# Two-layer metaformer on one core: layer 0's expert tiles store their results under the tile's own number, the fetches read only their image's part, and a power of the preparation runs on VectorE

## The chip, the cores and the metric

The kernel runs on one core of a Trainium2 chip. A core has five engines with instruction queues of their own, each worked off strictly in order: TensorE (PE in the profile; PEld is its weight load), VectorE (DVE), ScalarE (ACT), GpSimd (POOL) and SyncE (SP, which here only issues transfers). POOL also issues transfers: the indirect ones, which read or write one row per index, and here the stores of layer 0's results. The metric is the device time of one execution in microseconds; lower is better.

## What is computed

Four images of 256 channels by 32 x 32 pixels go through two layers. Layer 0 is a top-k attention with a depthwise convolution, added to its input, and then a mixture of experts: every token (pixel) goes to the two best of eight small two-matrix networks, and their weighted results are added to it. Layer 1 is a selective scan over four directions, prepared by a normalization and a softplus, added to its input, and then a second mixture of experts with wider networks.

```python
x = x + _L0_conv_ref(_ln_c(x), ...)          # attention
t = _to_tokens(x)
t = t + _L0_ffn_ref(_ln_t(t), ...)           # layer 0's experts, top 2 of 8
x = _from_tokens(t, x)
x = x + _L1_conv_ref(_ln_c(x), ...)          # selective scan, 16 states
t = _to_tokens(x)
x = _from_tokens(t + _L1_ffn_ref(_ln_t(t), ...), x)   # layer 1's experts
```

## The kernel before, in words

**Stages.** By the lines in the trace: attention up to about 1910 us, routing of layer 0 to 2050, layer 0's experts from 2050 to 2296, the scans to about 3563, layer 1's experts and the output to the end.

**Routing (L1123 to L1230, called at L1474 to L1490).** For each image DVE normalizes, finds the two best experts of each token, and counts. Each expert owns a region of 16 blocks of 256 rows in the DRAM tensor slots_x0; a token's slot is its expert's region plus its rank among that expert's tokens. The two slot numbers per token (slot0) are cast to integers, and POOL scatters the tokens there, 16 indirect transfers an image, two for each group of 128 tokens (L1486). After the last image, fill_in_phases (L1091) lays out the order of the tiles, 256 rows each: first those that hold tokens of image 0, then of image 1, then of images 2 and 3. Its constants make at most 15 tiles (FIRST) enough for image 0 and 23 (SECOND) for images 0 and 1; 36 tiles (USUAL) run always, three more only if needed.

**Layer 0's experts (Tile0, L1499 to L1566, loop at L1589).** For each tile SP loads its rows (xs, 6 buffers) and its expert's two matrices (4 buffers); PE transposes (tp, L1523) and DVE copies the result (xe, L1525); PE multiplies (hp, L1545), ACT applies Gelu (L1547), PE multiplies again (yp, L1553); DVE adds the bias (ys, 8 buffers, L1556), ACT scales (L1560), DVE adds the token itself where this is its best expert (L1561). POOL then reads the tile's block number into a register and stores ys to that block of slots_y0 (L1564), so that a result lies at the slot of its token.

**What runs beside the tiles (L1581 to L1600).** Two generators are advanced four steps after each tile. The first starts at tile 15: it fetches image 0's results by its slots (fetched, L1425: 8 plain indirect transfers for the tokens' first expert, then 8 that add the second one; four a step, so all within one tile), lets 20 steps pass, has PE transpose them (op, L1447) and DVE add them to x (L1454). Then it goes on with the preparation of image 0's scan (Prep.steps, L1332): mean (L1341), variance (L1353), the variance plus epsilon (ve, L1356), its power -0.5 on POOL (ln_r, L1359), one Newton step on DVE (ln_rr and ln_rs, L1361 to L1364), its spreading by PE (ln_rb, L1371), two projections (bp, zp), and a softplus in halves of 512 columns: Relu, Abs and Exp on ACT (L1405 to L1407) for each of four parts, rounding losses on DVE (lost, L1395), one Ln (L1411). The second generator starts at tile 23 and does for image 1 what the first began with. Images 2 and 3 are fetched during the first scans, one transfer at a time.

**What sets the order.** In this stage the framework orders the instructions of each engine: program order is the priority, and its own estimate of what is ready decides who goes first; it also puts in the waits, by the parts of tensors that instructions read and write. Where an address comes from a register or from indices, the part is whatever the slice that was handed over covers; slots_y0 was always handed over whole. In attention and scans the order is the program's, written out by hand; preparation of images 1 to 3 is advanced there twice a scan, beside POOL's products (uu, L1678, and da_c, L1711) and DVE's scans (h, L1691, L1700, L1717).

**Zeros.** Slots that no token fills must be finite, so SP fills slots_x0 and slots_y0 with zeros during attention (L831, at turns 20 and 36).

Of the kernel before, what the change touches and what calls it, by code (L numbers as in the profile page):

```python
# [52 lines left out]
WIN = 7  # L53
ROOT_BITS = float(0x1FBB4F2E)
WIDE = 256.0
FIRST_DVE = (3, 2)
# [5 lines left out]
def metaformer(ctx: ExitStack, tc: tile.TileContext, t: dict, out: bass.AP):  # L62
# [73 lines left out]
    slots_x0 = dram.tile([(E * BLOCKS + 1) * T, W0], F32, tag="slots_x0", name="slots_x0")  # L136
    slots_y0 = dram.tile([(E * BLOCKS + 1) * T, C], F32, tag="slots_y0", name="slots_y0")
    results = dram.tile([2 * B * L + 2 * P, C], F32, tag="results", name="results")
# [10 lines left out]
    with ExitStack() as st:  # L149
# [644 lines left out]
        with tc.manual_schedule():  # L794
            norms = [normed(b) for b in range(B)]
            gates = [gated(b) for b in range(B)]
            lead = [groups[0, 0].steps(pause=True), images[0].values(0)]

            def beside_norms():

                while lead[0] is not None:
                    went = next(lead[0], "end")
                    if went is None:
                        lead.append(lead.pop(0))
                        if lead[0] is None:
                            return
                    if went == "end":
                        lead[0] = None
                    if went is True:
                        return  # L810

            for i in range(B + 2):
                for b in range(B):
                    if 0 <= i - b < 3:
                        next(norms[b], None)
                if i >= 2:
                    beside_norms()
            for gate in gates:
                for _ in range(3):
                    next(gate, None)  # L820
                    beside_norms()
            while lead[0] is not None:
                beside_norms()
            aim, aim_lo, aim_hi, z, half_z, rate, ends = thresholds()
            for _ in lead[1]:
                pass
            start(0)
            for i in range(len(order) + 8):
                if i in (20, 36):
                    wide_by = W0 if i == 20 else C  # L830
                    nc.sync.dma_start((slots_x0 if i == 20 else slots_y0).rearrange("(a p) c -> p a c", p=P),  # L831
                                      zeros[:, :wide_by].unsqueeze(1).to_broadcast(
                                          [P, (E * BLOCKS + 1) * T // P, wide_by]))
                if i == 3:
                    nc.sync.dma_start(slots_x.rearrange("(a p) c -> p a c", p=P),
                                      zeros[:, :W].unsqueeze(1).to_broadcast([P, (E * BLOCKS + 1) * T // P, W]))
                turn(i)
            due(1 << 20)
# [221 lines left out]
    class Tiles:  # L1060
# [30 lines left out]
        def fill_in_phases(self, room, upto, psum, tag):  # L1091
# [11 lines left out]
            nc.vector.tensor_tensor(base, homes.rearrange("p k e -> p (k e)"), ends, ALU.subtract)  # L1103
            nc.vector.tensor_tensor(base, base, upto, ALU.add)
            nc.vector.tensor_tensor(leap[:, : V - 1], base[:, 1:], base[:, : V - 1], ALU.subtract)
            nc.vector.memset(leap[:, V - 1 :], float(E * BLOCKS))
# [15 lines left out]

    def route(b, layer, tok, slot, space, psum, tag):  # L1123

# [12 lines left out]
        wide = [P, NT, E]  # L1137
        eq, hot1, hot2 = room([NT, E]), room([NT, E]), room([NT, E])
        red, m1, m2 = room([NT]), room([NT]), room([NT])
# [61 lines left out]
        nc.vector.tensor_tensor(place, place, tote, ALU.subtract)  # L1201
        nc.vector.tensor_tensor(place, place, count.unsqueeze(2).to_broadcast([P, E, NT]), ALU.add)
        nc.vector.tensor_tensor(place, place, region.unsqueeze(2).to_broadcast([P, E, NT]), ALU.add)
        nc.vector.tensor_tensor(count, count, cum[:, :, NT - 1], ALU.add)
# [113 lines left out]
    dsk = load(sw, "dskip", [P, CT])  # L1318
    power = sw.tile([P, NT], F32, tag="power", name="power")
    nc.gpsimd.memset(power, -0.5)  # L1320

    class Prep:
# [9 lines left out]
        def steps(self, room, psum, tag):  # L1332
# [15 lines left out]
            for h in range(NHALF):  # L1348
# [8 lines left out]
                if h == 0:  # L1357
                    yield
            nc.gpsimd.tensor_tensor(r0, ve, power, ALU.pow)  # L1359
            yield  # L1360
            nc.vector.tensor_tensor(rr, r0, r0, ALU.mult)  # L1361
            nc.vector.tensor_tensor(rr, rr, ve, ALU.mult)
            nc.vector.tensor_scalar(rr, rr, -0.5, 1.5, ALU.mult, ALU.add)
            nc.vector.tensor_tensor(rs, r0, rr, ALU.mult)  # L1364
            yield
# [31 lines left out]

            for i, (c, cols) in enumerate(parts):
                zp = psum.tile([P, HALF], F32, tag=tag, name="zp")
                for k in range(CT):  # L1400
                    nc.tensor.matmul(zp, wd[:, k, ts(c, P)], xm[:, k, cols], start=(k == 0), stop=(k == CT - 1))
                if i:
                    lost(*parts[i - 1])
                yield
                nc.scalar.activation(self.delta[:, c, cols], zp, AF.Relu, bias=bd[:, c : c + 1])  # L1405
                nc.scalar.activation(v[:, c, cols], zp, AF.Abs, bias=bd[:, c : c + 1])
                nc.scalar.activation(v[:, c, cols], v[:, c, cols], AF.Exp, scale=-1.0)  # L1407
                yield
            lost(*parts[-1])
            yield  # L1410
            nc.scalar.activation(v, v, AF.Ln, bias=1.0)  # L1411
            yield
# [11 lines left out]

    def fetched(b, y, halves, times=1):  # L1425

        issued = 0
        for k in range(2):
            for h in halves:
                for i in range(4):  # L1430
                    n = b * NT + h * 4 + i
                    nc.gpsimd.indirect_dma_start(
                        out=y[h][:, i], out_offset=None, in_=slots_y0,
                        in_offset=bass.IndirectOffsetOnAxis(ap=slot0[:, k, n : n + 1], axis=0),
                        compute_op=ALU.add if k else ALU.bypass)
                    issued += 1
                    if issued % times == 0:
                        yield

# [17 lines left out]
    def pause(times):  # L1457
        for _ in range(times):
            yield

    with ExitStack() as st:
# [4 lines left out]
            "p (e d) -> p e d", e=E))  # L1466
        pw = st.enter_context(tc.tile_pool(name="m0_e", bufs=4))
        with ExitStack() as sr:
            pr = sr.enter_context(tc.tile_pool(name="r0_w", bufs=1))
# [3 lines left out]
            scattered = nc.alloc_semaphore("scattered")  # L1473
            for b in range(B):  # L1474
                d = pd.tile([P, CT, L], F32, tag="d", name="d")
                here = slot0[:, :, ts(b, NT)]
                for _ in norm(b, 0, tokens[b], pd, ps_n, "t", "t", d):
                    pass
                numbers = pr.tile([P, 1408], F32, tag="numbers", name="numbers")
                for _ in route(b, 0, tokens[b], here, numbers, ps_n, "t"):  # L1480
                    pass
# [14 lines left out]
        ps_h = st.enter_context(tc.tile_pool(name="m0_ps_h", bufs=2, space=PSUM))  # L1496
        blocks_x, blocks_y = (a.rearrange("(k a p) c -> k p a c", a=T // P, p=P) for a in (slots_x0, slots_y0))

        class Tile0:  # L1499
# [58 lines left out]
            def store(self):  # L1558
                for a in range(T // P):
                    nc.scalar.mul(self.ys[:, a], self.ys[:, a], self.wt[:, a : a + 1])  # L1560
                    nc.vector.scalar_tensor_tensor(self.ys[:, a], self.xs[:, a, :C], self.best[:, a : a + 1],  # L1561
                                                   self.ys[:, a], ALU.mult, ALU.add)
                block = self.register(1, E * BLOCKS, [mybir.EngineType.Pool])
                nc.gpsimd.dma_start(blocks_y[bass.ds(block, 1)].rearrange("o p a c -> p (o a) c"), self.ys)  # L1564

# [15 lines left out]
        def whole(b):  # L1581
            y = [pb.tile([P, 4, C], F32, tag=f"y{h}", name="y", bufs=1) for h in range(NHALF)]
            yield from fetched(b, y, range(NHALF), 4)
            yield from pause(20)
            for h in range(NHALF):
                yield from completed(b, h, y[h], ps_n, "t")

        beside = [(FIRST, chain(whole(0), preps[0].steps(room, ps_n, "t"))), (SECOND, whole(1))]
        for i in range(USUAL):  # L1589
# [4 lines left out]
            for first_tile, steps in beside:  # L1594
                if i >= first_tile:
                    for _ in range(4):
                        next(steps, None)
# [435 lines left out]
```

## Time and profile before

| what | us |
|---|---|
| three timed runs | 4144.05, 4151.52, 4140.24 (median 4144.05) |
| the profiled execution, its own time | 4158.95 |
| span of the profiled execution, first to last instruction | 4157.4 |
| busy in it: PE / DVE / ACT / POOL | 3535.8 / 3022.8 / 2833.1 / 1791.8 |
| mean granted TensorE clock | 0.871 of full speed |

The profiled execution took 14.9 us more than the median of the timed runs. A row of the timeline or of a group gives start, duration, engine, line, operation, what it wrote from what, and in square brackets how long the engine had been idle and what released it. A row of the waits gives who waited for whom: the sum, how often, and the longest. A row of the stretches gives busy time and number of instructions of PE, PEld, DVE, ACT and POOL, then the granted clock, the share of the transfer engines and GB/s.

### The profile page before, as it was taken

To read this page: it belongs to the slowest core of one execution; us is meant where nothing else is said; L and a number is where in the kernel's file an instruction comes from. 1 tells how busy PE (TensorE), PEld (TensorE's weight loads), DVE (VectorE), ACT (ScalarE), POOL (GpSimd) and SP (SyncE) were. 2 spreads that over 40 slices of the span, in tenths; PEclk is the share of its full clock that TensorE was granted. 3 is DMA by queue.
4 is the path that set the end of the run, shared out by engine and by line. 5 is a ranking of instruction groups with operands and counts; after the bars stand their busy time and mean duration, and the time that the engine had idled before them with its cause. 6 is when DMAs were issued, how large, how long until landed. Compare 5 with 4: busy or idle time off the path is not lost. (4 is left out here: it accounts for less than half of the span.)

```text
span 4157.4 us, 50283 instructions
## 1 busy us (share of the span) xinstructions
PE 3535.8 (85%) x17502; PEld 1959.7 (47%) x17502; DVE 3022.8 (73%) x5343; ACT 2833.1 (68%) x3809; POOL 1791.8 (43%) x1440
## 2 busy tenths in 40 slices
PE   8378888888888887865496899999999999999996
PEld 5134444444444434433374344444444434688885
DVE  2689898989998989893364789899899899411112
ACT  2889999999999999973334576667667677422222
POOL 0146454554454445552433656445445446221111
PEclk8568777787878877877698999999999999999997
DMA  9300093008200000001374343324333334655565
GB/s 289 92 1 1 1 262 80 1 1 270 68 1 1 11 1 1 11 1 35 129 220 116 127 118 121 111 95 125 116 98 120 118 102 136 189 184 184 189 196 182
DMA packets 274075, 426.38 MB, mean 103 GB/s; under 512 B 31889, under 2 KB 214418, under 8 KB 273682
## 3 DMA queue, kind: packets, MB, share of 16 engines
q1 hardware_dynamic: 250128, 373.22, 29.5%
q0 software_dynamic: 19904, 48.42, 3.6%
q8 instruction: 142, 2.33, 0.2%
q10 hardware_dynamic: 3778, 1.41, 0.1%
q14 instruction: 123, 1.01, 0.1%
HBM read 280.34 MB, written 142.64 MB: 102 GB/s over the span
## 5 line engine op out<-in xcount | busy, mean ns | idle before, releaser
L490 POOL TENSOR_SCALAR dr<-s_n,last 128x1024 bf16<-128x1024 f32 x256 | 732.0, 2877 | 863.4 <-DVE state L518 410.0
L406 ACT ACTIVATE junk_a<-s_n,state 128x1024 int8<-128x1024 f32 x448 | 514.8, 1149 | 28.1 <-DVE state L518 9.0
L1711 POOL TENSOR_TENSOR da_c<-prod,come 128x1024 f32<-128x1024 f32 x128 | 247.5, 1933 | 417.2 <-DVE h L1717 354.4
L410 DVE TENSOR_SCALAR_CACHE_REDUCE junk_v<-s_n,state 128x1024 int8<-128x1024 f32 x320 | 408.7, 1277 | 8.8
L1881 ACT ACTIVATE hid<-hp,b 128x256 f32<-128x256 f32 x288 | 133.8, 474 | 355.9 <-PE hp L1879 353.2
L457 DVE SCALAR_TENSOR_TENSOR w<-s_n,win 128x1024 f32<-128x1024 f32 x256 | 349.9, 1367 | 5.3
L460 DVE MAX8 win<-w 128x8 f32<-128x1024 f32 x256 | 314.5, 1228 | 8.8
L558 ACT ACTIVATE ex<-sT 128x1024 f32<-128x1024 f32 x256 | 247.1, 1016 | 93.5 <-PE sT L550 93.4
L1678 POOL TENSOR_TENSOR uu<-dx,bb 128x1024 f32<-128x1024 f32 x128 | 304.3, 2377 | 1.2 <-DMA bb<-bc_d 1.1
L406 ACT ACTIVATE junk_a<-s_n,guess 128x1024 int8<-128x1024 f32 x256 | 294.3, 1149 | 7.4
L1691 DVE TENSOR_TENSOR_SCAN h<-da,uu 128x1024 f32<-128x1024 f32 x128 | 290.8, 2272 | 4.3 <-POOL uu L1678 4.3
L1717 DVE TENSOR_TENSOR_SCAN h<-da_c,uu 128x1024 f32<-128x1024 f32 x128 | 291.1, 2274 | 0.0
L1700 DVE TENSOR_TENSOR_SCAN h<-da,uu 128x1024 f32<-128x1024 f32 x128 | 289.8, 2264 | 0.0
L568 PE MATMUL o_ps<-ex,vT 128*32 128x256 f32 x2048 | 242.8, 452 | 43.3 <-ACT ex L558 34.8
L1665 ACT ACTIVATE da_c<-delta,a_log 128x1024 f32<-128x1024 f32 x128 | 268.1, 2095 | 3.4 <-DMA slots_y<-ys 3.3
L1721 PE MATMUL hp<-h,ident 128*128 128x512 f32 x512 | 249.5, 610 | 21.8 <-DVE h L1717 21.6
L1879 PE MATMUL hp<-xe,w 128*128 128x256 f32 x1152 | 258.8, 381 | 7.0 <-DVE xe L1867 6.8
L1686 PE MATMUL hp<-h,twice 128*128 128x512 f32 x512 | 243.8, 599 | 19.3 <-DVE h L1691 19.1
L440 ACT COPY s_n<-sp 128x1024 f32<-128x1024 f32 x256 | 245.4, 1003 | 21.8 <-PE sp L432 11.4
L1679 ACT COPY uu<-uu 128x1024 f32<-128x1024 f32 x128 | 253.5, 1981 | 4.0 <-POOL uu L1678 4.0
L1887 PE MATMUL yp<-w2e,hid 128*128 128x256 f32 x1152 | 255.9, 379 | 0.0
L1890 DVE TENSOR_TENSOR ys<-yp,b2e 128x512 f32<-128x512 f32 x36 | 24.9, 692 | 317.3 <-PE yp L1887 317.3
(542 smaller groups left out, 7487.2 us busy)
## 6 DMA issues: line engine op xcount, KB each, us to landing
bb<-bc_d SPq DMA_DIRECT2D x128, 512.0 KB
cb<-bc_d SPq DMA_DIRECT2D x128, 512.0 KB
w<-in_w SPq DMA_DIRECT2D x36, 1024.0 KB
w2e<-in_w SPq DMA_DIRECT2D x36, 1024.0 KB
slots_x<-zeros SPq DMA_DIRECT2D x1, 33411.0 KB
slots_x<-zeros SPq DMA_DIRECT2D x1, 33282.0 KB
slots_y<-zeros SPq DMA_DIRECT2D x1, 33024.0 KB
w<-in_w SPq DMA_DIRECT2D x72, 256.0 KB
```

The costliest lines, as they stand in the source:

```text
L406: nc.scalar.activation(junk, self.row(r), AF.Sign, bias=thr, scale=-1.0, accum_out=u)
L410: nc.vector.tensor_scalar(junk, self.row(r), thr, None, ALU.is_lt, ALU.add, accum_out=u)
L457: nc.vector.scalar_tensor_tensor(w, self.row(r), self.win[:, r, 0:1], self.row(r), ALU.is_gt if r < LAST_DVE else ALU.is_ge, ALU.subtract, ...
L460: nc.vector.max(out=self.win[:, r, 1:], in_=w)
L490: ins = nc.gpsimd.tensor_scalar(dr, self.row(r), self.last[:, r : r + 1], None, ALU.is_lt)
L1665: nc.scalar.activation(grid(self.da_c), cols_flipped(self.prep.delta[:, self.c]), AF.Exp, scale=self.decay)
L1678: nc.gpsimd.tensor_tensor(self.uu[:, 0], self.prep.dx[:, self.c], self.bb, ALU.mult)
L1691: nc.vector.tensor_tensor_scan(rows.rearrange("p r w -> p (r w)"), self.da, self.uu[:, 0], 0.0, ALU.mult, ALU.add)
L1700: nc.vector.tensor_tensor_scan(hs[:, ::-1], self.da[:, ::-1], self.uu[:, 0][:, ::-1], 0.0, ALU.mult, ALU.add)
L1717: nc.vector.tensor_tensor_scan(hs, self.da_c, self.uu[:, 1], 0.0, ALU.mult, ALU.add)
L1879: nc.tensor.matmul(hp[:, f % 2], self.w1[:, c, ts(f, P)], self.xe[:, c], start=(c == 0), stop=(c == CT - 1))
L1887: nc.tensor.matmul(yp[:, a], self.hid[:, f, ts(a, P)], self.w2[:, f, :], start=(f == 0), stop=(f == NF - 1))
```

## The change

1. Results are stored by tile number: tile i writes rows 256 i to 256 i + 255 of rows_y0, a tensor of 39 tiles, at an address that the program knows; POOL reads no register for it.
2. To find a token's result, its rank and its two experts are kept from the routing (rank, hots), fill_in_phases keeps for each phase and expert where its tiles begin and where its ranks end, and a new generator, located, works out row numbers on DVE for all four images, beside the tiles from tile 1 on. The scatter's indices move to a tile of their own (here).
3. A fetch is handed only the first 15, 23 or 39 tiles of rows_y0. The order of the transfers is by half, then by expert; one is issued per step, four beside a tile. The pause shrinks from 20 steps to 8. The generators start one tile earlier.
4. The zero fill of the results covers three tiles, not 129 blocks.
5. The power -0.5 is replaced by an integer estimate and three Newton steps on DVE.
6. The softplus takes one Exp over all 2048 columns after the four parts, and the losses come after it, one part a step.

```diff
-    slots_y0 = dram.tile([(E * BLOCKS + 1) * T, C], F32, tag="slots_y0", name="slots_y0")
+    rows_y0 = dram.tile([NTILE * T, C], F32, tag="rows_y0", name="rows_y0")
...
-                if i in (20, 36):
-                    wide_by = W0 if i == 20 else C
-                    nc.sync.dma_start((slots_x0 if i == 20 else slots_y0).rearrange("(a p) c -> p a c", p=P),
-                                      zeros[:, :wide_by].unsqueeze(1).to_broadcast(
-                                          [P, (E * BLOCKS + 1) * T // P, wide_by]))
+                if i == 20:
+                    nc.sync.dma_start(slots_x0.rearrange("(a p) c -> p a c", p=P),
+                                      zeros[:, :W0].unsqueeze(1).to_broadcast([P, (E * BLOCKS + 1) * T // P, W0]))
+                if i == 36:
+                    nc.sync.dma_start(rows_y0[USUAL * T :].rearrange("(a p) c -> p a c", p=P),
+                                      zeros[:, :C].unsqueeze(1).to_broadcast([P, (NTILE - USUAL) * T // P, C]))
...
+            self.starts, self.limits = kept("starts", [PHASES, E]), kept("limits", [PHASES, E])
+            nc.vector.tensor_tensor(self.starts.rearrange("p k e -> p (k e)"), ends, upto, ALU.subtract)
+            nc.vector.tensor_scalar(self.starts, self.starts, float(T), None, ALU.mult)
+            nc.vector.tensor_scalar(self.limits.rearrange("p k e -> p (k e)"), upto, float(T), None, ALU.mult)
+            self.leaps = kept("leaps", [PHASES - 1, E])
+            nc.vector.tensor_tensor(self.leaps, self.starts[:, 1:], self.starts[:, : PHASES - 1], ALU.subtract)
...
-        nc.vector.tensor_tensor(place, place, count.unsqueeze(2).to_broadcast([P, E, NT]), ALU.add)
-        nc.vector.tensor_tensor(place, place, region.unsqueeze(2).to_broadcast([P, E, NT]), ALU.add)
+        rank = place if keep_rank is None else keep_rank
+        nc.vector.tensor_tensor(rank, place, count.unsqueeze(2).to_broadcast([P, E, NT]), ALU.add)
+        nc.vector.tensor_tensor(place, rank, region.unsqueeze(2).to_broadcast([P, E, NT]), ALU.add)
...
-            nc.gpsimd.tensor_tensor(r0, ve, power, ALU.pow)
-            yield
-            nc.vector.tensor_tensor(rr, r0, r0, ALU.mult)
-            nc.vector.tensor_tensor(rr, rr, ve, ALU.mult)
-            nc.vector.tensor_scalar(rr, rr, -0.5, 1.5, ALU.mult, ALU.add)
-            nc.vector.tensor_tensor(rs, r0, rr, ALU.mult)
+            nc.vector.tensor_scalar(r0.bitcast(I32), ve.bitcast(I32), -0.5, RSQRT_BITS, ALU.mult, ALU.add)
+            for src, dst in ((r0, rs), (rs, r0), (r0, rs)):
+                nc.vector.tensor_tensor(rr, src, src, ALU.mult)
+                nc.vector.scalar_tensor_tensor(rr, rr, -0.5, ve, ALU.mult, ALU.mult)
+                nc.vector.scalar_tensor_tensor(dst, rr, 1.5, src, ALU.add, ALU.mult)
...
-            for i, (c, cols) in enumerate(parts):
+            for c, cols in parts:
                 zp = psum.tile([P, HALF], F32, tag=tag, name="zp")
                 for k in range(CT):
                     nc.tensor.matmul(zp, wd[:, k, ts(c, P)], xm[:, k, cols], start=(k == 0), stop=(k == CT - 1))
-                if i:
-                    lost(*parts[i - 1])
                 yield
                 nc.scalar.activation(self.delta[:, c, cols], zp, AF.Relu, bias=bd[:, c : c + 1])
                 nc.scalar.activation(v[:, c, cols], zp, AF.Abs, bias=bd[:, c : c + 1])
-                nc.scalar.activation(v[:, c, cols], v[:, c, cols], AF.Exp, scale=-1.0)
                 yield
-            lost(*parts[-1])
+            nc.scalar.activation(v, v, AF.Exp, scale=-1.0)
             yield
+            yield
+            for part in parts:
+                lost(*part)
+                yield
...
-    def fetched(b, y, halves, times=1):
-
-        issued = 0
+    def located(b, hots, rank, room):
+
+        add, far = room([E, NT]), room([E, NT])
+        pick, at = room([NT, E]), room([NT])
+
+        def spread(v):
+            return v.unsqueeze(2).to_broadcast([P, E, NT])
+
+        nc.vector.tensor_tensor(add, rank, spread(every.starts[:, 0]), ALU.add)
+        for p in range(1, min(b, PHASES - 1) + 1):
+            nc.vector.tensor_tensor(far, rank, spread(every.limits[:, p - 1]), ALU.is_ge)
+            nc.vector.tensor_tensor(far, far, spread(every.leaps[:, p - 1]), ALU.mult)
+            nc.vector.tensor_tensor(add, add, far, ALU.add)
+        yield
         for k in range(2):
-            for h in halves:
+            nc.vector.tensor_tensor(pick, hots[k], add.rearrange("p e n -> p n e"), ALU.mult)
+            nc.vector.tensor_reduce(at, pick, AX.X, ALU.add)
+            nc.vector.tensor_copy(slot0[:, k, ts(b, NT)], at)
+            yield
+
+    def fetched(b, y, halves):
+
+        upto = (FIRST, SECOND, NTILE)[min(b, PHASES - 1)]
+        for h in halves:
+            for k in range(2):
                 for i in range(4):
                     n = b * NT + h * 4 + i
                     nc.gpsimd.indirect_dma_start(
-                        out=y[h][:, i], out_offset=None, in_=slots_y0,
+                        out=y[h][:, i], out_offset=None, in_=rows_y0[: upto * T],
                         in_offset=bass.IndirectOffsetOnAxis(ap=slot0[:, k, n : n + 1], axis=0),
                         compute_op=ALU.add if k else ALU.bypass)
-                    issued += 1
-                    if issued % times == 0:
-                        yield
+                    yield
...
-                here = slot0[:, :, ts(b, NT)]
+                here = pr.tile([P, 2, NT], I32, tag="here", name="here")
...
-                block = self.register(1, E * BLOCKS, [mybir.EngineType.Pool])
-                nc.gpsimd.dma_start(blocks_y[bass.ds(block, 1)].rearrange("o p a c -> p (o a) c"), self.ys)
+                nc.gpsimd.dma_start(rows_y0[ts(self.i, T)].rearrange("(a p) c -> p a c", p=P), self.ys)
...
-            yield from fetched(b, y, range(NHALF), 4)
-            yield from pause(20)
+            yield from fetched(b, y, range(NHALF))
+            yield from pause(8)
...
+        def places():
+            for b in range(B):
+                yield from located(b, hots0[b], rank0[b], lambda shape: pb.tile(
+                    [P, *shape], F32, tag=f"at{len(shape)}", name="at", bufs=4))
+
+        beside = [(2, places()), (FIRST, chain(whole(0), preps[0].steps(room, ps_n, "t"))), (SECOND, whole(1))]
         for i in range(USUAL):
...
-                if i >= first_tile:
+                if i >= first_tile - 1:
```

More of the change, by code (lines that the diff above doesn't have):

```diff
@@ L54 @@
 ROOT_BITS = float(0x1FBB4F2E)
+RSQRT_BITS = float(0x5F3759DF)
 WIDE = 256.0
@@ L1121, in metaformer, with route @@
     extra = rt.tile([1, 1], I32, tag="extra", name="extra")
-    def route(b, layer, tok, slot, space, psum, tag):
+    def route(b, layer, tok, slot, space, psum, tag, keep_hots=None, keep_rank=None):
         used = 0
@@ L1137, in route @@
         wide = [P, NT, E]
-        eq, hot1, hot2 = room([NT, E]), room([NT, E]), room([NT, E])
+        eq, hot1, hot2 = room([NT, E]), *(keep_hots or (room([NT, E]), room([NT, E])))
         red, m1, m2 = room([NT]), room([NT]), room([NT])
@@ L1318, in metaformer @@
     dsk = load(sw, "dskip", [P, CT])
-    power = sw.tile([P, NT], F32, tag="power", name="power")
-    nc.gpsimd.memset(power, -0.5)
     class Prep:
@@ L1467, in metaformer @@
         pw = st.enter_context(tc.tile_pool(name="m0_e", bufs=4))
+        hots0, rank0 = [], []
         with ExitStack() as sr:
@@ L1474, in metaformer @@
             for b in range(B):
+                hots0.append([wp.tile([P, NT, E], F32, tag=f"hot{b}{k}", name="hot") for k in range(2)])
+                rank0.append(wp.tile([P, E, NT], F32, tag=f"rank{b}", name="rank"))
                 d = pd.tile([P, CT, L], F32, tag="d", name="d")
-                here = slot0[:, :, ts(b, NT)]
+                here = pr.tile([P, 2, NT], I32, tag="here", name="here")
                 for _ in norm(b, 0, tokens[b], pd, ps_n, "t", "t", d):
@@ L1479, in metaformer @@
                 numbers = pr.tile([P, 1408], F32, tag="numbers", name="numbers")
-                for _ in route(b, 0, tokens[b], here, numbers, ps_n, "t"):
+                for _ in route(b, 0, tokens[b], here, numbers, ps_n, "t", hots0[b], rank0[b]):
                     pass
@@ L1496, in metaformer @@
         ps_h = st.enter_context(tc.tile_pool(name="m0_ps_h", bufs=2, space=PSUM))
-        blocks_x, blocks_y = (a.rearrange("(k a p) c -> k p a c", a=T // P, p=P) for a in (slots_x0, slots_y0))
+        blocks_x = slots_x0.rearrange("(k a p) c -> k p a c", a=T // P, p=P)
         class Tile0:
@@ L1582, in whole @@
             y = [pb.tile([P, 4, C], F32, tag=f"y{h}", name="y", bufs=1) for h in range(NHALF)]
-            yield from fetched(b, y, range(NHALF), 4)
-            yield from pause(20)
+            yield from fetched(b, y, range(NHALF))
+            yield from pause(8)
             for h in range(NHALF):
                 yield from completed(b, h, y[h], ps_n, "t")
-        beside = [(FIRST, chain(whole(0), preps[0].steps(room, ps_n, "t"))), (SECOND, whole(1))]
+        def places():
[3 more added lines that the diff above has]
+        beside = [(2, places()), (FIRST, chain(whole(0), preps[0].steps(room, ps_n, "t"))), (SECOND, whole(1))]
         for i in range(USUAL):
```

## The prediction

> **What bounds the kernel now.** I began with the page's chain of waits: it reaches back only to 3563 us, into layer 1's experts, which this change leaves alone. So I read the change's own stage, 2050 to 2296, in stretches.
>
> ```profile
> 2050.00:2100.00 50.00, 43.12 (x194) 34.58 (x195) 28.51 (x88) 17.12 (x38) 5.83 (x8) 0.89 0.79 243
> 2100.00:2150.00 50.00, 43.60 (x208) 35.21 (x206) 31.15 (x93) 17.86 (x41) 16.96 (x19) 0.96 0.79 235
> 2150.00:2200.00 50.00, 43.76 (x196) 34.67 (x194) 24.92 (x69) 15.35 (x33) 17.20 (x17) 0.87 0.66 180
> 2200.00:2250.00 50.00, 24.30 (x89) 15.07 (x90) 16.37 (x43) 14.56 (x22) 22.53 (x19) 0.73 0.40 95
> 2250.00:2300.00 50.00, 31.38 (x150) 24.42 (x149) 34.46 (x87) 30.93 (x47) 8.79 (x10) 0.93 0.36 114
> ```
>
> PE carries the stage with 43 to 44 of 50 us, then loses half of the fourth stretch, and its clock falls. The waits of the stage say why:
>
> ```profile
> PEld hp L1545 <- DVE xe L1525: 30.3, 2, 29.5
> DVE ln_rr L1361 <- POOL ln_r L1359: 29.8, 1, 29.8
> PE hp L1545 <- DVE xe L1525: 29.5, 2, 29.1
> ...
> POOL slots_y L1564 <- DMA slots_y<-ys: 17.4, 6, 3.8
> ```
>
> PE waited 29.1 us for a copy on DVE (xe), and DVE 29.8 us for the power on POOL. The timelines of POOL, DVE and PE show the queueing:
>
> ```profile
> 2197.12 1.02 POOL L1432 DMA_INDIRECT y<-slots_y,slot  x1 [5.60 <-DMA slots_y<-ys]
> ...
> 2220.20 1.54 POOL L1432 DMA_INDIRECT y<-slots_y,slot  x1 [0.30 <-issue]
> 2221.18 2.28 POOL L1359 TENSOR_TENSOR ln_r<-ln_ve,power 128x8 f32<-128x8 f32 x1
> ```
>
> ```profile
> 2192.97 0.69 DVE L1556 TENSOR_TENSOR ys<-yp,b2e 128x512 f32<-128x512 f32 x1 [0.95 <-PE yp L1553]
> 2223.49 0.17 DVE L1361 TENSOR_TENSOR ln_rr<-ln_r 128x8 f32<-128x8 f32 x1 [29.83 <-POOL ln_r L1359]
> ```
>
> ```profile
> 2224.63 1.22 PE L1545 MATMUL hp<-xe,w 128*128 128x256 f32 x2 [29.09 <-DVE xe L1525]
> ```
>
> The power's input was ready at 2183, but it stood behind image 1's sixteen fetches, which themselves waited 5.6 us for a store to land. The next tile's xe stood behind ln_rr on DVE, and PE behind xe. An undisturbed tile takes 4.35 us (stores at 2092.58, 2096.92).
>
> **The parts, one by one.** Minus is time saved.
>
> *Power to VectorE, layer 0.* Nothing of the preparation is left on POOL, so the 29.1 us of PE go. Next late there is nothing: the transposes for xe had ended by 2194, and fetched rows of image 1 are wanted only five tiles later. PE's clock is 0.50 to 0.69 from 2205 to 2230; the matmuls after the wait, busy 5.00 us of 2225 to 2230 at 0.69, regain some 2 us. DVE gets ten instructions of 128x8 for four (which ran at 0.2 us apart): 6 x 0.2 = +1.2, on the path, as PE's spreading waits for the result. Together **-29.9**.
>
> *Power to VectorE, scans.* Three more powers (1.68 us each) hold POOL before da_c:
>
> ```profile
> 2744.12 1.68 POOL L1359 TENSOR_TENSOR ln_r<-ln_ve,power 128x8 f32<-128x8 f32 x1 [5.62 <-DVE ln_ve L1356]
> ```
>
> ```profile
> 2747.75 1.98 PE L1686 MATMUL hp<-da_c,ident 128*128 128x512 f32 x4 [2.09 <-POOL da_c L1711]
> ```
>
> PE, busy 94% of the scans, loses 2.1 us each time; DVE's ten new instructions stand before a scan instead (+1.2). 3 x (1.2 - 2.1) = **-3**, between -6 and 0.
>
> *One Exp.* Now four Exp drag eight table loads beside Gelu:
>
> ```profile
> 2240.52 1.28 ACT L1407 ACT_TABLE_LOAD   x1
> 2241.82 0.63 ACT L1407 ACTIVATE sp<-sp 128x512 f32<-128x512 f32 x1
> 2242.47 1.28 ACT L1547 ACT_TABLE_LOAD   x1
> ```
>
> Six loads go: 6 x 1.28 = 7.7, and four Exp of 0.63 become one of about 1.91 (the Ln of that shape): 8.3 us less of ACT, which is busy without a gap from 2240 to 2265. But PE is idle only some 3.3 us in that stretch and 2.1 just after, so 5.4 is the most; and the long Exp holds Gelu for 1.28 + 1.91 + 1.28 at one go. I take **-3**, between -5.4 and 0. In the scans no Gelu stands between; 0.
>
> [...]
>
> *Row numbers (located).* Instructions on DVE: 1 + 4 + 7 + 7 for the four images, and 2 x 3 for each of the four: 43. The routing runs such 128x64 instructions 0.25 us apart: 10.8 us in tiles 1 to 3. DVE idles about 1.4 us a tile (3.3 busy of 5), which hides 4.2; up to 6.6 is left. The planner may push some into later tiles: **+4**, between 0 and 7.
>
> *Routing.* Four more instructions of 0.2 us in fill_in_phases, and the last scatter starts right behind that chain (DVE's L1113 ends at 2029.08, POOL starts at 2029.07): **+0.7**. The tile "here" adds a wait: image 1's casts (1971.04) must wait for image 0's scatter, with the next image's subtractions behind them on DVE. The scatter's last issue ended at 1967.9, and one of its kind lands in 2.65 us (a row of the chain): done at 1970.6, before the cast. 0.
>
> *Stores.* They no longer wait for one another (17.4 us in the waits above) nor for a register, but eight ys buffers already hid that: PE never waited for it. 0; if that cover were thin, it is a gain of at most 17.
>
> *Zero fill.* 33 MB leave attention at 959. The five turns under it (964.15 to 1091.2, by the last instruction of POOL's check) last 24.4 to 26.9, the others 23.9 to 33.1: it cost nothing. 0.
>
> *Fetch of image 0.* Now it begins one tile earlier, in four groups of four between stores. During the first fetch today DVE, ACT and PE stop together twice (PE busy 2.95 and 2.34 of 5 from 2140 to 2150), and tiles 17 to 19 lose 17.3 - 2 x 4.35 = 8.6 us. I keep that: the number of transfers is the same. The new order has one tight place: a group of plain transfers takes 4 x 1.26 = 5.0, an adding one 4 x 1.85 = 7.4, three stores between about 1 each. From 2134 the last group ends at 2162 and lands about 2165, while PE reaches its transposes after tile 21 at 2158 without the stops, at 2167 with them. So a wait of 6.5 where the stops are absent and none where they stay: **+2**.
>
> *Fetch of image 1.* Its 16 transfers ran while everything else stood still. Now tiles run beside them, and the same stops can show: 0 to 8.6, **+5**. Its landing is no issue: 28 us of POOL's time from tile 22, against six tiles of 5 to 6 us until PE wants it.
>
> [...]
>
> **Sum.** -29.9 - 3 - 3 + 4 + 0.7 + 2 + 5 = -24.2, say -25. The profiled execution's 4158.95 us become 4134. It lay 14.9 above the median of the runs shown, 4144.05, from which the same 25 give **4119**.
>
> **Rivals.**
>
> *More comes back.* Both stops vanish as the fetches spread (-8.6, and the +5 goes), tables and scans give all: -30.3 - 5.4 - 6 - 8.6 + 1 = -49, so 4095. For it: idle PE also lowers its clock. Against: transfers still come 1.26 apart.
>
> *The stall is replaced.* DVE's row numbers (+7), stops in both fetches (+8.6) or PE at the tight place (+6.5), nothing from tables or scans: -29.9 + 0.7 + 7 + 8.6 + 6.5 = -7, so 4137. Its hard end is that the planner puts another waiting instruction before xe; I see none that waits as long.
>
> *Waits by the whole tensor, slower.* If the narrowed slices do not narrow the waits, each group of four waits for the store ahead to land (4.0: issue at 2131.71, fetch at 2135.73) and each store for the group (5.25 in the timeline at 2165.88). POOL then needs 24.8 + 4 x 9.2 = 62 us an image, against 26 of cover for image 0 and 36 for image 1: PE waits 36 + 26 = 62, less the 25 won and the 2 + 5 counted: +30, so 4174. It decides from about 2.5 us a group on. Against it: the store's address is now known, and the slices are cut at tiles. That would also be the change not doing what it says.
>
> **Chances.** Forecast (4106 to 4131) 0.56, more comes back (below 4106) 0.19, the stall replaced (4131 to 4150) 0.15, whole-tensor waits 0.10. The range takes all terms at their good ends, about -50, and at their bad ones, -7, so 4094 to 4137, and 3 us more on each side for the spread of the timed runs: 4090 to 4140; it leaves out the slower rival and the outer parts of the two beside the forecast. About 0.3% (12 us) is what a measurement of this kernel can tell from no change: faster by more 0.75, within 0.14, slower 0.11.
>
> **What would show it.** Right: no tensor instruction of POOL between the fetches; PE's longest wait for xe under 5 us; ten short DVE instructions after ln_ve; two table loads for Exp where there were eight; the 2.1 us before da_c gone three times; stores that wait for DVE only. Wrong: PE waiting for y at the transposes, POOL waiting for stores inside a fetch, tiles 1 to 3 over 6 us, or stops of all engines in the second fetch beyond 9 us.

## The result: no change that can be measured, and the profile after

| | before | after |
|---|---|---|
| timed runs, median | 4151.94 us (12 runs, 4140.24 to 4170.11) | 4156.61 us (12 runs, 4142.98 to 4169.16) |
| ratio of after to before, 95% interval | | 1.0007 [0.9985, 1.0029] |
| profiled execution, own time / span | 4158.95 / 4157.4 us | 4149.70 / 4148.0 us |

A gain of 25 us was forecast (0.994), and it lies outside the interval. To see where it went, I cut both profiled executions at four points that every kernel here has: the first IOTA of the routing, the end of the last scatter before layer 0's experts, and the first and the last product uu of the scans.

| stretch, us | before | after | difference |
|---|---|---|---|
| attention | 1916.9 | 1906.3 | -10.6 |
| routing | 132.1 | 134.9 | +2.8 |
| layer 0's experts | 250.4 | 220.5 | -29.9 |
| scans | 1246.8 | 1276.7 | +29.9 |
| from the last uu to the end | 611.2 | 609.7 | -1.5 |

The first two rows tell nothing: over the twelve kernels profiled in this study attention ended between 1899 and 1922 us and the routing took 125 to 143, also where nothing in them was different. The experts won 29.9 us, 8 more than the terms on record for this stage add up to (-21.9), and the scans gave the same amount back.

The experts' stretches of after, in the columns of before (PE, PEld, DVE, ACT, POOL, clock, transfers):

```profile
2050.00:2100.00 50.00, 47.78 (x222) 38.39 (x221) 33.99 (x117) 18.35 (x42) 7.23 (x10) 0.97 0.82 248
2100.00:2150.00 50.00, 46.49 (x225) 37.33 (x223) 34.74 (x102) 19.14 (x44) 22.88 (x22) 1.00 0.87 251
2150.00:2200.00 50.00, 42.41 (x183) 29.79 (x184) 26.08 (x72) 15.72 (x32) 30.12 (x27) 0.93 0.68 175
2200.00:2250.00 50.00, 42.41 (x196) 32.10 (x196) 36.81 (x98) 26.40 (x45) 6.44 (x9) 1.00 0.42 133
```

The fourth stretch has PE at 42 us where it had 24 and the clock at 1.00 where it had 0.73; in all four the clock stays above 0.9. Of PE's waits in this stage, the two that the prediction named:

```profile
PE op L1472 <- DMA y<-rows_y,slot: 5.1, 4, 2.1
PE hp L1573 <- DVE xe L1553: 2.6, 3, 0.9
```

The 29 us for xe are gone; the small wait for fetched rows is the "tight place" of the prediction. On ACT, one Exp stands between two table loads where four had eight:

```profile
2206.31 1.28 ACT L1412 ACT_TABLE_LOAD   x1
2207.61 1.91 ACT L1412 ACTIVATE sp<-sp 128x2048 f32<-128x2048 f32 x1
...
2210.33 1.28 ACT L1575 ACT_TABLE_LOAD   x1
```

Now the scans. The group of the products uu (minimum, median and maximum in ns, then first and last start in us) gives their length in every kernel, here before and after:

```profile
L1678 POOL TENSOR_TENSOR uu<-dx,bb x128: 2340/2362/2977, 2299.4 to 3546.1; 128x1024 f32<-128x1024 f32 x128
```

```profile
L1710 POOL TENSOR_TENSOR uu<-dx,bb x128: 2337/2357/2386, 2261.6 to 3538.3; 128x1024 f32<-128x1024 f32 x128
```

One uu is issued per turn, so its 128 starts cut the scans into 127 turns; turn n is the one that ends with the nth start. Turns without a preparation beside them agree to 0.1 us between the two kernels (turns 107 to 128, of the last image: 9.53 and 9.45, 8.97 and 8.97, and so on). The 29.9 us lie in the turns with a preparation and the few just behind its end: 5.3 up to turn 28 (beside image 0's scans), 13.5 up to turn 67 (image 1's), 11.3 up to turn 99 (image 2's). The first of them in image 1's scans is turn 46 (13.59 us against 11.74), where the power is. DVE of after in that turn:

```profile
2711.60 1.35 DVE L1366 TENSOR_SCALAR ln_r<-ln_ve 128x8 int32<-128x8 int32 x1
...
2714.59 0.17 DVE L1370 SCALAR_TENSOR_TENSOR ln_rs<-ln_rr,ln_r 128x8 f32<-128x8 f32 x1
2714.68 2.28 DVE L1723 TENSOR_TENSOR_SCAN h<-da,uu 128x1024 f32<-128x1024 f32 x1
```

POOL and PE of after beside it:

```profile
2711.01 1.91 POOL L1743 TENSOR_TENSOR da_c<-prod,come 128x1024 f32<-128x1024 f32 x1 [4.99 <-DVE h L1749]
```

```profile
2717.11 2.65 PE L1718 MATMUL hp<-h,twice 128*128 128x512 f32 x4 [2.14 <-DVE h L1723]
```

The first and the last of the four Newton instructions of before, and what DVE did next:

```profile
2750.51 0.14 DVE L1361 TENSOR_TENSOR ln_rr<-ln_r 128x8 f32<-128x8 f32 x1
...
2751.10 0.17 DVE L1364 TENSOR_TENSOR ln_rs<-ln_r,ln_rr 128x8 f32<-128x8 f32 x1
2751.18 2.28 DVE L1717 TENSOR_TENSOR_SCAN h<-da_c,uu 128x1024 f32<-128x1024 f32 x1
```

Two things are to be seen. All ten instructions of after stand ahead of the forward scan L1723, and PE waits 2.14 us for that scan; before, the four Newton instructions stood ahead of the column scan L1717, and PE had no wait behind them. And the first of them, 128x8, takes 1.35 us: it begins while POOL multiplies da_c and ends at 2712.95, 0.03 us after POOL.

**The theory (A).** The generator of a preparation is advanced twice a turn: a first half (the loop at L1763 of before, ahead of third) whose DVE work falls between the column scan and the next forward scan, and a second half (the loop at L1801 of before, behind come_in) whose DVE work falls ahead of the column scan. A `yield` ends a half. The change took one `yield` away behind the power and added five at the softplus. So from the power to the softplus every step stands in the other half, where DVE is late and POOL's da_c is running, and the whole preparation ends four steps, two turns, later. **Rivals:** the price of the new instructions wherever they stand (B), the single Exp (C), the later end alone (D).

### The profile page after: what moved, and what is told of

Read it like the earlier page. It is cut to its first block, busy times and chain, and to the rows that moved or that the text cites. A ratio compares the mean times of both kernels' runs of the same rounds, so it can differ in the third digit from the quotient of the medians.

```text
span 4148.0 us, 50218 instructions
## 1 busy us (share of the span) xinstructions
PE 3522.9 (85%) x17502; PEld 1945.6 (47%) x17502; DVE 3045.6 (73%) x5414; ACT 2824.3 (68%) x3791; POOL 1779.8 (43%) x1435
## 3 DMA queue, kind: packets, MB, share of 16 engines
q1 hardware_dynamic: 217872, 340.19, 27.1%
## 5 line engine op out<-in xcount | busy, mean ns | idle before, releaser
L1723 DVE TENSOR_TENSOR_SCAN h<-da,uu 128x1024 f32<-128x1024 f32 x128 | 290.5, 2270 | 4.7 <-POOL uu L1710 4.7
L1705 ACT ACTIVATE da<-delta,a_log 128x1024 f32<-128x1024 f32 x128 | 143.0, 1118 | 210.3 <-DVE h L1732 210.3
L1701 ACT ACTIVATE prod<-cum,a_log 128x1024 f32<-128x1024 f32 x128 | 146.8, 1147 | 161.4 <-POOL da_c L1743 161.3
```

The lines of the kernel that those rows point to most:

```text
L1723: nc.vector.tensor_tensor_scan(rows.rearrange("p r w -> p (r w)"), self.da, self.uu[:, 0], 0.0, ALU.mult, ALU.add)
```

## The experiments

All lengths are of scans and experts as cut above, from one profiled execution each; ratios are of timed runs. Of the scans a length repeats to about 0.5 us (e4 against before below).

**e1: the step put back ahead of the power, softplus in four parts.**

```diff
+            yield
             nc.vector.tensor_scalar(r0.bitcast(I32), ve.bitcast(I32), -0.5, RSQRT_BITS, ALU.mult, ALU.add)
...
-            nc.scalar.activation(v, v, AF.Exp, scale=-1.0)
-            yield
-            yield
-            for part in parts:
-                lost(*part)
-                yield
+                if i:
+                    lost(*parts[i - 1])
...
+                nc.scalar.activation(v[:, c, cols], v[:, c, cols], AF.Exp, scale=-1.0)
...
+            lost(*parts[-1])
+            yield
```

> The changed kernel with one step put back ahead of the ten instructions for the power, and with the softplus in four parts as before: every step of the preparation stands in the half of a turn where it stood before. Measures: the scans from the first to the last product uu (before 1246.8 us, after 1276.7) and layer 0's experts from the end of the last scatter to the first uu (250.4 and 220.5). Theory A (the place: the 30 us come back in the scans because a missing step moves the preparation into the other half of the turn, where POOL's da_c and the next scan stand in its way): scans 1238 to 1247, experts 220 to 225, the whole 30 us under the kernel before (ratio 0.992). Theory B (the price: the new instructions themselves are dearer, wherever they stand): the power's ten instructions are still there, so scans 1265 or more and the ratio above 0.997.

Measured: scans 1242.3 us, experts 218.9 (a little under the range), 4118.45 us (median of 6 runs), ratio **0.9928 [0.9902, 0.9953]**. Theory A; B falls: the ten instructions are there and the scans are shorter than before by 4.5. In turn 46 (10.41 us) the same first instruction, now in the second half:

```profile
2709.77 0.14 DVE L1367 TENSOR_SCALAR ln_r<-ln_ve 128x8 int32<-128x8 int32 x1
```

**e2: only the softplus in four parts; the step behind the power stays missing** (the second part of e1's diff alone).

> The changed kernel with the softplus in four parts as before, and nothing else: the step behind the power is still missing, so now all of the preparation behind the power, the last four steps of dx and delta too, stands in the other half of a turn. Theory A (the place): the scans stay long, 1270 to 1300 us, although the single long Exp and its four extra steps are gone. Theory C (the single Exp and its five extra steps are the cause): scans 1247 to 1255.

Measured: scans **1320.0 us**, experts 221.4. C falls. With the single Exp away, the steps Ln, dx and delta stand in the wrong half too, and it is worse than A's range: 73 us over before. Turns 57 to 63 take 10.77 to 10.79 us each, where before has 9.32 and then 9.11 to 9.19.

**e3: the kernel before with only the power on VectorE, its step kept.**

```diff
-            nc.gpsimd.tensor_tensor(r0, ve, power, ALU.pow)
             yield
-            nc.vector.tensor_tensor(rr, r0, r0, ALU.mult)
...
+            nc.vector.tensor_scalar(r0.bitcast(I32), ve.bitcast(I32), -0.5, RSQRT_BITS, ALU.mult, ALU.add)
...
```

> The kernel before with only the power on VectorE, its step kept: stores, fetches, zero fill and softplus are those of before. By the terms on record: layer 0's experts 250.4 less 30, 220 us, and scans 1246.8 less 3 (between 1240.8 and 1246.8). Rival: the wait for the power is replaced by image 1's fetch, whose sixteen transfers still stand in one row on POOL behind the stores: experts 235 us or more.

Measured: experts 223.3 us, scans 1241.7, 4119.16 us (median of 4 runs), ratio 0.9911 [0.9883, 0.9939]. The two terms of the power hold: -27.1 in the experts (forecast -29.9) and -5.1 in the scans (forecast -3, bounds -6 and 0). This one edit, alone, gains as much as e1, which has the others beside it; the two intervals overlap.

**e4: the changed kernel with the power back on POOL and the softplus in four parts.**

```diff
-            nc.vector.tensor_scalar(r0.bitcast(I32), ve.bitcast(I32), -0.5, RSQRT_BITS, ALU.mult, ALU.add)
...
+            nc.gpsimd.tensor_tensor(r0, ve, power, ALU.pow)
+            yield
+            nc.vector.tensor_tensor(rr, r0, r0, ALU.mult)
...
```

> The changed kernel with the power back on POOL and the softplus in four parts as before: row numbers, stores by tile and spread fetches remain. The preparation is that of before, so the scans take 1246.8 us within 0.5 by theory A. Layer 0's experts: by the terms on record the power still waits behind image 1's transfers, and row numbers and fetches cost some 11 us more: 255 to 262 us. Rival: the spread fetches alone undo the wait, since POOL takes the power between two groups of four: 220 to 232 us.

Measured: scans 1247.2 us, as A has it, and experts **217.8**: my number (255 to 262) failed and the rival won. POOL of e4, with the power between two transfers of image 1's fetch:

```profile
2184.67 0.95 POOL L1461 DMA_INDIRECT y<-rows_y,slot  x1 [0.30 <-issue]
2185.63 1.71 POOL L1368 TENSOR_TENSOR ln_r<-ln_ve,power 128x8 f32<-128x8 f32 x1
2187.53 1.01 POOL L1461 DMA_INDIRECT y<-rows_y,slot  x1 [0.19 <-issue]
```

and what DVE still waited for it:

```profile
DVE ln_rr L1370 <- POOL ln_r L1368: 3.8, 1, 3.8
```

Because a fetch is now issued one transfer a step, the power gets its turn after four transfers, not after sixteen. The spread fetch and the move of the power each take away the same wait of 30 us; the second adds nothing in this stage. (e4 also keeps the stores by tile, the narrowed slices and the earlier start, so the rows show how the power gets in, and not what the spreading alone is worth.)

**e5: as e1, but the step behind the ten instructions**, so that they alone stand in the first half.

```diff
-            yield
             nc.vector.tensor_scalar(r0.bitcast(I32), ve.bitcast(I32), -0.5, RSQRT_BITS, ALU.mult, ALU.add)
...
                 nc.vector.scalar_tensor_tensor(dst, rr, 1.5, src, ALU.add, ALU.mult)
+            yield
```

> The same as e1_late_parts, but the step is put behind the ten instructions of the power and not ahead of them: all else stands in its old half, and only the power's own instructions stand in the other half, ahead of a forward scan and beside POOL's da_c. Theory A (the place): each of the three powers costs 2 to 3 us there (turn 46 took 13.59 us in the changed kernel and 10.41 in e1), so the scans take 1248 to 1251 us against 1242.3 in e1. Theory B (the price of the instructions): no difference, 1242 to 1243.

Measured: scans 1248.9 us (+6.6 over e1), turn 46 13.60 and turn 78 13.60. The same instructions, half a turn earlier, cost 2.2 us each time over all.

**e6 and e7: the kernel before with one, and with two, empty steps at the head of the preparation.**

```diff
             sq = room("ln_sq", [CT, L])
+            yield
             for h in range(NHALF):
```

> The kernel before, unchanged but for one empty step at the head of the preparation: every one of its steps comes half a turn later. Not one instruction is added or removed. Theory A (the half of the turn decides): scans 1300 to 1335 us against 1246.8. Theory D (what costs is that the preparation ends later): within 3 us of 1246.8.

> The kernel before with two empty steps at the head of the preparation: every step comes a whole turn later and stands in its old half. Theory A: scans within 6 us of 1246.8. Theory D: longer than with one empty step.

Measured: scans **1313.0 us with one, 1254.3 with two**. The group uu of e6:

```profile
L1679 POOL TENSOR_TENSOR uu<-dx,bb x128: 2338/2358/2968, 2292.9 to 3606.0; 128x1024 f32<-128x1024 f32 x128
```

Not an instruction differs from before, and 66 us are lost; one more empty step gives 59 of them back. D falls: twice the delay costs less. The 7.5 us of e7 are 1.5 more than I allowed; 1.3 of them is in each of the turns 65 and 97 (11.30 each against 10.03), where the end of the preparation meets the cumulative scan (cum).

**e8: e2, with POOL filling da_c where it multiplied.**

```diff
-                nc.gpsimd.tensor_tensor(grid(self.da_c), self.prod[:, :HW, :],
-                                        self.come.unsqueeze(2).to_broadcast([P, HW, HW]), ALU.mult)
+                nc.gpsimd.memset(self.da_c, 0.0)
```

> The kernel of e2_parts_only, in which POOL only fills da_c with zeros instead of multiplying prod by come: the carried-in part of the column scans is left out, and POOL reads nothing from SBUF at that place. In e2 a DVE instruction of 0.69 us took 2.28 us beside that product and ended 0.55 us after it, and the turns 55 to 63 took 10.78 us against 9.12 to 9.18 before. Theory A with a lock (DVE's instructions with two SBUF inputs wait until POOL's reading instruction has ended): these instructions take 0.7 us again and the turns 9.1 to 9.3, scans 1250 to 1290 us. Rival (place in DVE's queue alone, without a lock): they keep the turn at 10.4 or more, scans above 1305.

Measured: scans 1264.6 us against 1320.0, turns 57 to 63 9.12 to 9.19. First after, where the losses are in the first half (POOL, then DVE):

```profile
2834.08 1.93 POOL L1743 TENSOR_TENSOR da_c<-prod,come 128x1024 f32<-128x1024 f32 x1 [3.31 <-DVE h L1749]
```

```profile
2834.28 2.28 DVE L1402 TENSOR_TENSOR dx<-sp,dx 128x512 f32<-128x512 f32 x1
```

then e8 in a turn of the same kind (POOL, then DVE):

```profile
2854.88 0.95 POOL L1742 MEMSET da_c<- 128x1024 f32 x1 [1.90 <-DVE h L1747]
```

```profile
2855.43 0.69 DVE L1422 TENSOR_TENSOR delta<-delta,dx 128x512 f32<-128x512 f32 x1
```

In after, DVE's instruction begins 0.20 us behind POOL's and ends 0.55 behind its end: it waited. In e8 one of the same shape begins inside POOL's instruction and takes its usual 0.69; the longest of all sixteen losses (L1402) is 0.693 us in e8 and 2.282 in e2. The filling is also half as long as the product (0.95 us for 1.9), so not all of the 55 us belong to that wait. Where no preparation runs, e8 is 0.8 us shorter than e2 in turns 29 to 43 and 1.1 in turns 100 to 128; at that rate the shorter instruction alone would give an estimated 5 to 7 us in all 127 turns. The filling, which only writes, did not hold up this instruction with its two inputs: the two overlap by 0.40 us. The integer estimate, which has one input, ran longer beside the filling all the same (POOL, then DVE, in e8):

```profile
2702.52 0.95 POOL L1742 MEMSET da_c<- 128x1024 f32 x1 [4.91 <-DVE h L1747]
```

```profile
2703.16 0.34 DVE L1366 TENSOR_SCALAR ln_r<-ln_ve 128x8 int32<-128x8 int32 x1
```

It took 0.34 us where it takes 0.17 undisturbed, and ended 0.03 behind the filling.

**e9 and e10: e1 with the single Exp left in,** in e9 with the changed kernel's losses, one a step, in e10 with two at a time in the second half.

```diff
             nc.scalar.activation(v, v, AF.Exp, scale=-1.0)
             yield
-            yield
             for part in parts:
                 lost(*part)
                 yield
```

> The changed kernel with the step put back ahead of the power, as in e1, but with the single Exp and its separate losses left in (one empty step behind Exp taken out, so that Ln and the last steps fall into their old half): two of the four losses still stand in the other half, beside POOL's da_c, and the preparation ends two turns later, with its last dx and delta beside the cumulative scan of turn 64. Against e1 (1242.3 us) by the account of the changed kernel's turns: the losses 2 x 2.1, the end 2.7, the long Exp up to 1.2, so 7 to 8 for each of two preparations and some 5 for the one in image 0's scans: scans 1258 to 1264 us. If the single Exp cost nothing in the scans, as the prediction had it: 1242 to 1245.

> As e9, but the losses come two at a time, in the half where they stood before; the number of steps is the same. Only the later end and the long Exp are left: 2.7 and up to 1.2 for a preparation, scans 1249 to 1254 us. If not the half but the separate losses themselves cost: as long as e9.

Measured: scans 1261.2 us in e9 and 1250.9 in e10, both inside the forecast; experts 215.1 and 215.6. The differences of successive kernels divide up the way of the scans from 1246.8 to 1276.7 (they add up to the whole by construction):

| term | from | us |
|---|---|---|
| the three powers leave POOL | e1 - before | -4.5 |
| later end, the long Exp, and losses two at a time | e10 - e1 | +8.6 |
| two of four losses in the first half | e9 - e10 | +10.4 |
| missing step: power, its spreading, the projections and Exp in the other half | after - e9 | +15.4 |
| sum | | +29.9 |

Of the 29.9, the wait beside POOL is a part only: in after six of the sixteen losses (2.28 to 2.93 us for 0.69) and two of the four estimates (1.35 for 0.17) ran long beside POOL, 12.5 us in all. The rest is not resolved into single instructions.

## Why the prediction was wrong

**The step that failed** is the pricing of the scans: "DVE's ten new instructions stand before a scan instead (+1.2). 3 x (1.2 - 2.1) = -3", and, of the single Exp, "In the scans no Gelu stands between; 0". Both count instructions. The diff also takes away the `yield` behind the power and puts five in at the softplus, and in a program whose order is written out by these steps that is an edit of its own. It was not in the sum at all, in none of the rivals, and it is worth +34.4 (the last three rows of the table; the first of them also holds the long Exp, which no run separates). The sum of -3 came out as +29.9.

**What was right.** That the 29 us of PE's wait are the power behind sixteen transfers, and that they go: experts -29.9, for a net of -21.9 in the sum (-29.9 power, -3 Exp, +4 row numbers, +7 fetches). That the stage came out at the very figure of the power's term, and that the scans lost the same 29.9, is chance: these are different sums. The price of the powers in the scans, with the step kept: -4.5 (e1) and -5.1 (e3) for -3. No POOL tensor instruction between the fetches, a longest wait for xe of 0.9, two table loads for Exp.

**What was mis-sized.**
- *Power, layer 0.* Right as an effect of the edit alone (e3), but not the cause it was given in the changed kernel: the fetch as changed had already undone the wait (e4). I priced the fetches as a cost of +7 and did not ask what they did to the wait of the next term.
- *Row numbers*, forecast +4: from tile 0's last result to tile 10's is 44.6 us after (2056.8 to 2101.3) and 44.3 before (2064.5 to 2108.8), so 0.3. The first instructions of it ran at 2045, behind 20 us in which DVE had nothing to do, and while the first tile's rows were still being loaded.
- *Fetch of image 0*, forecast +2: tiles 15 to 21 take 34.0 us after and 34.4 before. The stops of all engines at tiles 17 to 19 did not come back (22.6 us from tile 15 to 20, against 30.3), and the tight place stood in for them at tile 21, 11.4 us with 5.1 of waiting for y. It was put down as one or the other; so it was, at a sum near 0.
- *Fetch of image 1*, forecast +5: from tile 21 to 35 after takes 95.4 us and e3, whose fetch is that of before, 97.7. There is no cost to be seen; this also holds the Exp.
- *One Exp*, forecast -3: the experts take 216.8 to 221.4 with four Exp (e1, e2, e5, e8) and 215.1 to 220.5 with one (e9, e10, after): -1.7 between the means, inside the scatter.
- *Routing* and *zero fill*, forecast +0.7 and 0: neither can be told within the 18 us and 23 us over which these stretches vary. This stays open.

**A better kernel.** e1, which is the change with the step put back and the softplus as before, is 0.7% faster than before, and e3, the power alone, 0.9%; their intervals overlap, so neither is shown to be the better. Against the changed kernel e1 wins 34.4 us in the scans of the profiled executions.

## What to carry to other kernels

Where work is interleaved by generators, a `yield` is an instruction of the schedule: count those that a change adds and removes, and look at which slot every later step falls into, before pricing a single instruction. If the slots alternate, an odd number shifts everything behind it; two slots of the same turn can be worlds apart, here 66 us for one empty step. And when two edits attack the same wait, price each with the other already done.

## What was not expected of the hardware

Of the sixteen losses of after, which read two tensors from SBUF (the on-chip memory that holds the kernel's tiles), six ran beside da_c, for which POOL reads SBUF too. All six ended 0.54 to 0.56 us behind da_c: five that began 0.19 to 0.27 us after it took 2.28 us, one that began 0.45 us ahead of it 2.93; the other ten took 0.67 to 0.75. The integer estimate, of 128x8 and with a single input, went from 0.17 to 1.35 there, and to 0.34 beside the filling. In e8, where POOL only writes da_c, the longest of the sixteen losses took 0.693 us, and delta<-delta,dx, with two inputs from SBUF and begun inside the filling, took 0.69. With one input in PSUM (where the kernel keeps PE's results) xm<-x,ln_mean was not held up: it took 0.68 to 0.69 us in the ten of sixteen cases of after in which da_c was running. Why the one engine holds up the other, no row shows.

The reverse is on record too. In before's scans each of the nine transfers that POOL began inside a DVE scan with two SBUF inputs (eight times h<-da_c,uu, once cum<-inner,delta) ended 0.79 to 1.38 us behind that scan (DVE, then POOL):

```profile
2373.93 2.27 DVE L1717 TENSOR_TENSOR_SCAN h<-da_c,uu 128x1024 f32<-128x1024 f32 x1
```

```profile
2373.35 1.05 POOL L1432 DMA_INDIRECT numbers<-slots_y,slot  x1 [0.17 <-issue]
2374.71 2.28 POOL L1432 DMA_INDIRECT numbers<-slots_y,slot  x1 [0.30 <-issue]
```

These nine of the 32 transfers took 1.95 to 2.91 us, the other 23 took 0.95 to 1.61. One that began inside h<-da,uu, whose da is in PSUM, took 1.01 (at 2301.89). In the experts' stage of before nothing of the kind is to be seen: beside a DVE at work on the tiles the eight plain transfers took 0.95 to 1.05 us and the eight adding ones 1.53 to 1.74 (image 0, 2135.73 to 2160.63), beside an idle one 0.94 to 1.02 and 1.53 to 1.59 (image 1, 2197.12 to 2221.74).
